# A two-layer decoder's last stage: expert tiles of 128 tokens, sorted in halves of 64, with products by halves of the array

## The chip, the cores and the metric

The kernel runs on one core of a Trainium2 chip. TensorE (PE) multiplies, VectorE (DVE), ScalarE (ACT) and GpSimd (POOL) do the element work, and SyncE (SP) starts most of the transfers. The metric is the device time of one execution in microseconds. An execution under the profiler is also given by its span, from the first to the last instruction.

## The reference

A decoder of two layers works on `x`, 8 sequences of 256 tokens with 256 features, all in float32. Each layer is self-attention, cross-attention and a feed-forward part. Only the last feed-forward part, a mixture of eight experts beside one shared expert, is concerned by the change:

```
a = b * s                                   # 2048 tokens
scores_aE = x_aD @ router_DE                # 8 experts
vals_aK, idx_aK = jax.lax.top_k(scores_aE, 1)
gates_Ea = sigmoid(scores of the chosen expert, -inf for the others).T
routed_in_EaD = gates_Ea[:, :, None] * x_aD[None, :, :]
mid_EaF = silu(routed_in_EaD @ w1_eDF) * (routed_in_EaD @ w3_eDF)      # F = 704
routed_out_EaD = mid_EaF @ w2_eFD
shared_aD = silu(x_aD @ ws1_DF) * (x_aD @ ws3_DF) @ ws2_FD
out_aD = shared_aD + routed_out_EaD.sum(axis=0)
```

`x_aD` is the layer norm of `x`, and the result is added to `x`. Each token has one expert, so a kernel can sort the tokens by expert and give each expert its own tokens only.

## The kernel before

`plain` holds the whole computation. Its earlier stages (self- and cross-attention of layer 0, layer 0's experts, layer 1's self-attention, then `null_cross_attention`) take about 1175 us of the span. The change touches them in two places: `expert_tables` (line 493 on) fills two DRAM tables with zeros, and `reciprocals` (line 979) computes one over the softmax sums of layer 1's cross-attention and counts, in a column of `fit` for each batch, how many lie in a safe range. If a sum anywhere is out of range, a second, general program runs behind this one; `odd_i` carries that flag.

The last stage is `token_experts` (line 1082). It has four parts.

**Routing.** From the scores `sc` (tokens on partitions, 16 columns of 128 tokens) DVE finds each token's expert as a one-hot `hot`. Two matmuls (lines 1153 and 1154) count tokens, `run` adds the counts up over the 16 columns, `over` and `tiles` give each expert's number of 128-token tiles, and `at` the tile at which each expert begins. `pos_i` is each token's row in a table sorted by expert, in which every expert begins at a fresh tile, and `exp_i` is the expert of each tile. With eight experts up to 23 tiles can be needed (`SLOTS`).

**Scatter and shared expert.** GpSimd scatters the normed and gated tokens to their rows in the DRAM table `xs` with 16 indirect transfers (line 1205). Meanwhile PE works on the shared expert: `quarter(q)` makes the hidden layer of 512 tokens, and `joined` multiplies it out and adds it to `x`. Quarters 0 and 1 have their hidden layer from the stage before; quarter 2 is made here, and quarter 3 after the tiles. Behind these comes a small test over `dens`, the softmax sums of the other three attentions, and `fit` (lines 1223 to 1237).

**Tiles.** `slots` walks over the tiles, 19 always and the others behind two branches on the number that is filled. For each tile:

- `fetched(t)` (line 1239) has SP load the tile's 128 rows `xr` (waiting for all 16 scatters), read the tile's expert number, and fetch that expert's weights: `w13`, two transfers of 704 KB and a copy of the last 64 columns by GpSimd (line 790), and `w2`, one of 640 KB and one of 64 KB (lines 799 and 800). Two PE transposes and an ACT copy turn `xr` into `xrT`.
- `into` calls `hidden` (line 818): 11 blocks of 128 weight columns, each multiplied with the tile's 128 tokens in two steps (line 825), then silu on ACT and a product on DVE into `mid_r`.
- `outof` calls `outward` (line 1100): six products over the hidden layer against `w2`'s 256 columns, a copy by ACT, and a store to the DRAM table `ye`, which ACT starts.

The order on PE is written by hand: `fetched(t + 2)`, `into(t + 1)`, `outof(t)`. Weights have three buffers of each kind. SP runs its instructions in order, so a transfer that waits for its buffer holds back those behind it.

**Return.** GpSimd gathers each token's result from `ye` (line 1298) while PE makes quarter 3 of the shared expert; DVE adds, and SP stores the output.

A helper that the change brings into the tiles is already used in the earlier stages: `product` (line 168) issues one product as two, of 64 output partitions each, on the two halves of the array.

Of the kernel before, what the change touches and what calls it, by code (L numbers as in the profile page):

```python
# [50 lines left out]
SLOTS = NT + E - 1  # L51
NEG = -1.0e30
# [14 lines left out]
def plain(ctx: ExitStack, tc: tile.TileContext, a: dict, out: bass.AP, odd_i: bass.AP):  # L67
# [69 lines left out]

    xs = dram.tile([SLOTS * P, D], F32, name="xs")
    ye = dram.tile([SLOTS * P, D], F32, name="ys")

# [350 lines left out]
    def expert_tables():  # L491
        nc.sync.dma_start(gate, a["L0_ffn_gate_w"].rearrange("(c p) e -> p c e", p=P))
        nc.gpsimd.dma_start(experts, a["L0_ffn_experts"].rearrange("e (c p) f -> p e c f", p=P))
        zero = one.tile([P, D], F32, name="zero")
        nc.gpsimd.memset(zero, 0.0)
        nc.gpsimd.dma_start(xs.rearrange("(s p) d -> p s d", p=P), zero.unsqueeze(1).to_broadcast([P, SLOTS, D]))
        nc.gpsimd.dma_start(
            ye[19 * P :].rearrange("(s p) d -> p s d", p=P), zero.unsqueeze(1).to_broadcast([P, SLOTS - 19, D])
        )

        key_i = one.tile([P, E, TOP], I32, name="key_i")
        nc.gpsimd.iota(key_i, [[1, E], [E, TOP]], base=0, channel_multiplier=0)
        key = one.tile([P, S], F32, name="key")
        nc.vector.tensor_copy(key, key_i.rearrange("p e r -> p (e r)"))
        kps = mm.tile([P, 2, 2 * P], F32, tag="mm", name="kps")
        keycol = one.tile([P, 2], F32, name="keycol")
        for h in range(2):
            nc.tensor.transpose(kps[:, h, :P], key[:, bass.ts(h, P)], ident)
        nc.vector.tensor_copy(keycol, kps[:, :, 0])
        for h in range(2):  # L510
            nc.vector.tensor_scalar(later[:, h, :], key, keycol[:, h : h + 1], None, ALU.is_gt)
        num_i = one.tile([P, S], I32, name="num_i")
        nc.gpsimd.iota(num_i, [[1, S]], base=0, channel_multiplier=0)
        nc.vector.tensor_copy(num, num_i)
# [134 lines left out]
    def weights_x():  # L649
# [3 lines left out]
        ctxs = ctx.enter_context(tc.tile_pool(name="ctxs", bufs=2, side="right"))  # L653
        wproj = ExitStack()
        wp = wproj.enter_context(tc.tile_pool(name="wp", bufs=1, side="right"))
# [117 lines left out]
    fit = const.tile([P, B], F32, name="fit")  # L773

    w_l0.close()

# [41 lines left out]
    def hidden(mid, w13, cols, pair, silu):  # L818

        n = cols.shape[2]  # L820
        for i in range(NFC):
            h1, h3 = pair(n)
            for h, lo in ((h1, i * P), (h3, FF + tail + i * P))[: 2 if i < full else 1]:
                for c in range(2):
                    nc.tensor.matmul(h, w13[:, c, lo : lo + P], cols[:, c, :], start=c == 0, stop=c == 1)  # L825
            fw = P
            if i == full:
                fw, h1, h3 = tail, h1[:tail], h1[tail:]
            sl = silu(n)[:fw]
            nc.scalar.activation(sl, h1, AF.Silu)  # L830
            yield nc.vector.tensor_tensor(mid[:fw, i, :n], sl, h3, ALU.mult)  # L831

# [31 lines left out]
    def null_cross_attention(phase):  # L864
# [135 lines left out]

        def divide(oT, rs):
# [29 lines left out]
        def quarter(q):  # L1031
            return hidden(shared["mid_s"][q], shared["ws13"], shared["xnT"][:, :, bass.ts(q, 2 * S)], pair, silu)
# [8 lines left out]
        for b in range(B):  # L1041
# [13 lines left out]
            rs, old = reciprocals(b, den, en), en  # L1055
            if more:
# [25 lines left out]
    def token_experts(phase):  # L1082
        one = phase.enter_context(tc.tile_pool(name="e1", bufs=1))
        work = phase.enter_context(tc.tile_pool(name="e2", bufs=2))
        wts = phase.enter_context(tc.tile_pool(name="e3", bufs=3))
# [3 lines left out]
        xnT, ws13, ws2, mid_s = (shared[n] for n in ("xnT", "ws13", "ws2", "mid_s"))  # L1089

        mid_r = [ended(one.tile([P, NFC, P], F32, name=f"midr{i}")) for i in range(2)]
        w2_r = [ended(one.tile([P, NFC, D], F32, name=f"w2{i}")) for i in range(3)]
# [14 lines left out]
        def quarter(q):  # L1107
            mid = mid_s[q % 2]
            for last in hidden(mid, ws13, xnT[:, :, bass.ts(q, 512)], pair, silu):
                pass  # L1110
            return mid, last
# [5 lines left out]
        mids = [*mid_s]  # L1117


        def row(n, step, name):  # L1120
            i = one.tile([P, n], I32, name=f"{name}_i")
            nc.gpsimd.iota(i, [[step, n]], base=0, channel_multiplier=0)
# [3 lines left out]

        ecol, tcol, jcol = row(E, -1, "ecol"), row(SLOTS, 1, "tcol"), row(NT, P, "jcol")
        nc.vector.tensor_scalar(ecol, ecol, float(E), None, ALU.add)
# [28 lines left out]
        for j in range(NT):  # L1157
            nc.vector.tensor_tensor(run[:, j + 1, :], run[:, j, :], count[:, j, :], ALU.add)
        over = one.tile([P, E, NT], F32, name="overe")
        nc.vector.tensor_tensor(  # L1160
            over,
            run[:, NT, :].unsqueeze(2).to_broadcast([P, E, NT]),
            jcol.unsqueeze(1).to_broadcast([P, E, NT]),
            ALU.is_gt,
        )
        tiles = one.tile([P, E], F32, name="tiles")
        nc.vector.tensor_reduce(tiles, over, AX.X, ALU.add)
        at = one.tile([P, E + 1], F32, name="at")
        nc.vector.memset(at[:, 0:1], 0.0)
        for e in range(E):  # L1170
            nc.vector.tensor_tensor(at[:, e + 1 : e + 2], at[:, e : e + 1], tiles[:, e : e + 1], ALU.add)
        filled_i = one.tile([P, 1], I32, name="filled_i")
        nc.vector.tensor_copy(filled_i, at[:, E : E + 1])
        rows = one.tile([P, E], F32, name="rowse")
        nc.vector.tensor_scalar(rows, at[:, :E], float(P), None, ALU.mult)
        nc.vector.tensor_tensor(run[:, :NT, :], run[:, :NT, :], before, ALU.add)
        nc.vector.tensor_tensor(
            run[:, :NT, :], run[:, :NT, :], rows.unsqueeze(1).to_broadcast([P, NT, E]), ALU.add
        )
        nc.vector.tensor_tensor(run[:, :NT, :], run[:, :NT, :], hot, ALU.mult)  # L1180
        pos = one.tile([P, NT], F32, name="pos")
        nc.vector.tensor_reduce(pos, run[:, :NT, :], AX.X, ALU.add)
        nc.vector.tensor_scalar(pos, pos, SLOTS * P - 1.0, None, ALU.min)
        pos_i = one.tile([P, NT], I32, name="pos_i")
        nc.vector.tensor_copy(pos_i, pos)
        past = one.tile([P, SLOTS, E - 1], F32, name="past")
        nc.vector.tensor_tensor(
            past,
            tcol.unsqueeze(2).to_broadcast([P, SLOTS, E - 1]),
            at[:, 1:E].unsqueeze(1).to_broadcast([P, SLOTS, E - 1]),  # L1190
            ALU.is_ge,
        )
        exp_f = one.tile([P, SLOTS], F32, name="exp_f")
        nc.vector.tensor_reduce(exp_f, past, AX.X, ALU.add)
        exp_i = one.tile([P, SLOTS], I32, name="exp_i")
# [20 lines left out]
        for q in range(3):  # L1216
# [6 lines left out]
            alld = dens.rearrange("p k t h -> p (k t h)")  # L1223
        inside = one.tile([P, 3 * NT * H], F32, name="inside")
        nc.vector.tensor_scalar(inside, alld, 1.0e-25, None, ALU.is_ge)
        nc.vector.scalar_tensor_tensor(inside, alld, 1.0e25, inside, ALU.is_le, ALU.mult)
        ends = one.tile([P, 1], F32, name="ends")
        nc.vector.tensor_reduce(ends, inside, AX.X, ALU.min)
        low = one.tile([P, 2], F32, name="lowe")
        nc.vector.tensor_reduce(low[:, 1:2], fit, AX.X, ALU.min)  # L1230
        nc.vector.tensor_scalar(low[:, 1:2], low[:, 1:2], S - 0.5, None, ALU.is_gt)
        nc.vector.tensor_copy(low[:, 0:1], ends)
        fine = mm.tile([P, 2 * D], F32, tag="mm", name="fine")[:, :2]
        nc.tensor.matmul(fine, ones, low, start=True, stop=True)
        total = one.tile([P, 1], F32, name="total")
        nc.vector.tensor_reduce(total, fine, AX.X, ALU.add)
        nc.vector.tensor_scalar(odd_i, total, 2 * P - 0.5, None, ALU.is_lt)

        def fetched(t):
# [4 lines left out]
            e = nc.sync.value_load(exp_i[0:1, t : t + 1], min_val=0, max_val=E - 1)  # L1244

            def of(n):
                return a[f"L1_ffn_{n}"][bass.ds(e, 1), :, :].rearrange("a p d -> (a p) d")

            w13 = w_in(wts, of("w1_eDF"), of("w3_eDF"), "w13")
            w2 = w_out(w2_r[t % 3], of("w2_eFD"))  # L1250
# [5 lines left out]
            return w13, w2, xrT  # L1256

        def into(t, w13, w2, xrT):
            mid = mid_r[t % 2]
            for _ in hidden(mid, w13, xrT, pair, silu):  # L1260
                pass
            return mid, w2

        def outof(t, mid, w2):
            yr = work.tile([P, D], F32, tag="yr", name="yr")
            nc.scalar.copy(yr, outward(mid, w2, 0))
            nc.scalar.dma_start(ye[bass.ts(t, P), :], yr)

        def slots(lo, hi):


            with tc.manual_schedule(engines={mybir.EngineType.PE}):
                got = {lo: fetched(lo), lo + 1: fetched(lo + 1)}
                ahead = into(lo, *got.pop(lo))
                for t in range(lo, hi):
                    now = ahead
                    if t + 2 < hi:
                        got[t + 2] = fetched(t + 2)
                    if t + 1 < hi:
                        ahead = into(t + 1, *got.pop(t + 1))  # L1280
                    outof(t, *now)


        slots(0, 19)
        filled = nc.values_load(filled_i[0:1, 0:1], min_val=NT, max_val=SLOTS)
        with tc.If(filled > 19):
            slots(19, 21)
            with tc.If(filled > 21):
                slots(21, SLOTS)
# [964 lines left out]
```

## Time and profile before

| | |
|---|---|
| Time, median of 3 runs | 1417.21 us (1416.78 to 1418.94) |
| Profiled execution | 1420.55 us, span 1418.5 us, granted clock 0.992 |
| Scatters to `xs` on POOL | 1193.28 to 1213.4 us of the span |
| First weights sent by SP | 1191.94 us |
| First transpose of a tile | 1227.3 us |
| Last product out of a tile ends | 1374.8 us |
| Quarter 3 of the shared expert begins | 1376.79 us |
| Last product of the span ends | 1408.6 us |

In the page and the answers that follow, a group of instructions is named by line, engine, operation, output and inputs, then the shape. "128*128" after a matmul is the part of the array that it uses (rows * columns), so "128*64" uses half of the columns. A float32 product appears as two records. PE is the multiplying, PEld the loading of weights beside it. A timeline line gives the start, the length and the number of instructions merged into it. A line of windows gives the stretch, its length, the busy time of PE, PEld, DVE, ACT and POOL with the number of instructions, the granted clock, the share of time in which the core's DMA engines were busy, and GB/s.

### The profile page before, as it was taken

What the parts mean: (1) busy time and instruction counts of PE and PEld (TensorE: products, weight loads), DVE (VectorE), ACT (ScalarE), POOL (GpSimd) and SP (SyncE); (2) the same over time, 40 slices, a digit from 0 to 9 for tenths busy, and PEclk for the clock granted to TensorE, in tenths of its full rate; (3) what the DMA queues carried; (4) which work ended last, traced back from release to release, by engine and by line L of the source; (5) the groups of instructions that cost most, each with busy time, mean ns of one, the idle gap of its engine ahead of it and who ended that gap; (6) DMA issues with size and microseconds to landing.
All of it is one profiled execution on the core that took longest, in us unless ns stands there. A gap on an engine that the chain in (4) does not pass through costs nothing. (4 is left out here: it accounts for less than half of the span.)

```text
span 1418.5 us, 23533 instructions
## 1 busy us (share of the span) xinstructions
PE 1372.8 (97%) x9514; PEld 974.4 (69%) x9514; DVE 498.9 (35%) x1477; ACT 462.9 (33%) x754; POOL 387.1 (27%) x487
## 2 busy tenths in 40 slices
PE   6999999999999999999999999999999999999997
PEld 3666756756766666676677767667677656799974
DVE  6343553653655744410131312122131325222212
ACT  2555444444443434423131313223131311132220
POOL 4132142142143244212141424324141523100013
PEclk8999999999999999999999999999999999999999
DMA  9000000000000005010101101010101103589943
GB/s 306 27 12 16 16 17 8 16 16 1 2 9 1 9 1 216 2 62 16 45 2 44 31 15 31 15 31 16 31 2 30 30 0 128 182 302 318 314 134 110
DMA packets 54553, 91.05 MB, mean 64 GB/s; under 512 B 6160, under 2 KB 38720, under 8 KB 52896
## 3 DMA queue, kind: packets, MB, share of 16 engines
q1 hardware_dynamic: 47360, 70.00, 15.8%
q0 software_dynamic: 4064, 16.13, 3.1%
q10 hardware_dynamic: 3008, 3.28, 0.6%
q8 instruction: 79, 1.29, 0.4%
q14 instruction: 42, 0.34, 0.1%
HBM read 79.03 MB, written 10.37 MB: 63 GB/s over the span
## 5 line engine op out<-in xcount | busy, mean ns | idle before, releaser
L260 PE MATMUL o<-pT,padv 128*64 128x256 f32 (+1 forms) x1536 | 171.6, 365 | 1.1 <-POOL pT L240 1.1
L237 ACT ACTIVATE pT<-st 128x1024 f32<-128x1024 f32 (+1 forms) x128 | 110.7, 916 | 88.7 <-PE st L228 87.9
L260 PEld LDWEIGHTS o<-pT,padv 128*64 128x64 f32 x1536 | 103.1, 137 | 52.6 <-issue 10.1
L228 PE MATMUL st<-qm,kT 64*128 64x256 f32 (+1 forms) x1024 | 117.2, 367 | 1.6 <-DVE qm L206 1.4
L874 PE MATMUL fm<-ctxT,wkv_x 128*128 128x256 f32 x512 | 112.1, 379 | 0.0
L897 PE MATMUL vps<-wkv_x,ctxT 128*128 128x512 f32 x256 | 111.7, 594 | 0.0
L228 PEld LDWEIGHTS st<-qm,kT 64*128 64x128 f32 x1024 | 90.0, 189 | 26.8 <-issue 15.1
L874 PEld LDWEIGHTS fm<-ctxT,wkv_x 128*128 128x128 f32 x512 | 96.6, 190 | 12.8
L825 PE MATMUL h<-xrT,w 128*128 128x128 f32 x836 | 96.6, 275 | 0.2 <-ACT xrT L1255 0.2
L825 PEld LDWEIGHTS h<-xrT,w 128*128 128x128 f32 x836 | 94.9, 192 | 0.5 <-ACT xrT L1255 0.5
L933 POOL TENSOR_TENSOR both<-pTx 128x512 f32<-128x512 f32 x64 | 79.4, 1272 | 52.1 <-ACT pTx L931 33.0
L931 ACT ACTIVATE pTx<-stx 128x1024 f32<-128x1024 f32 x64 | 62.1, 1023 | 90.0 <-PE stx L927 90.0
L897 PEld LDWEIGHTS vps<-wkv_x,ctxT 128*128 128x128 f32 x256 | 48.2, 190 | 57.5 <-issue 57.4
L237 ACT ACTIVATE pT<-st,kbias 128x1024 f32<-128x1024 f32 x64 | 68.1, 1115 | 28.7 <-PE st L228 28.6
L830 ACT ACTIVATE sl<-h 128x128 f32<-128x128 f32 (+1 forms) x126 | 38.8, 308 | 115.6 <-PE h L825 106.7
L152 POOL TENSOR_TENSOR lnrs<-lnve,mhalf 128x2 f32<-128x2 f32 x48 | 34.0, 710 | 154.3 <-DVE lnve L150 102.8
L831 DVE TENSOR_TENSOR midr<-sl,h 128x128 f32<-128x128 f32 x114 | 32.9, 288 | 109.9 <-ACT sl L830 61.1
L228 PE MATMUL st<-qm,memk 64*128 64x256 f32 x512 | 68.8, 393 | 0.5
L927 PE MATMUL stx<-qTx,kTx 64*128 64x256 f32 x512 | 64.3, 391 | 2.5 <-ACT pTx L931 2.5
L147 DVE BATCH_NORM_STATS2 lxst<-yx 128x6 f32<-128x256 f32 x16 | 6.0, 418 | 162.1 <-ACT yx L1015 162.1
L170 PE MATMUL qk<-l_wqkv,xnT 128*64 128x512 f32 x256 | 62.3, 608 | 0.7 <-ACT xnT L180 0.7
L240 POOL TENSOR_SCALAR_AFFINE_SELECT pT<-pT 128x512 f32<-128x512 f32 x64 | 40.1, 646 | 81.8 <-ACT pT L237 78.5
(260 smaller groups left out, 2125.9 us busy)
## 6 DMA issues: line engine op xcount, KB each, us to landing
w<-L_ffn_w_eDF SPq DMA_DIRECT2D x38, 704.0 KB
w<-L_ffn_w_eFD SPq DMA_DIRECT2D x19, 640.0 KB
rs<-rd SPq DMA_DIRECT2D x16, 512.0 KB
ctxT<-ctx_T SPq DMA_DIRECT2D x8, 512.0 KB
wkv_x<-L_xattn_Wkv POOLq DMA_DIRECT2D x1, 4096.0 KB
xs<-zero POOLq DMA_DIRECT2D x1, 2944.0 KB
xr<-xs SPq DMA_DIRECT2D x19, 128.0 KB
ys<-yr ACTq DMA_DIRECT2D x19, 128.0 KB
```

The source lines that it names most:

```text
L170: nc.tensor.matmul(out[h], lhsT[:, h], rhs, start=start, stop=stop, skip_group_check=True)
L228: nc.tensor.matmul(st[:, g, i, :n], kT[rows, c, bass.ts(kt, P)], qm[rows, 2 * mq + i, c, q0:], start=True, stop=True,)
L237: nc.scalar.activation(pT[:, :, :, :n], st[:, :, :, :n], AF.Exp, scale=scale, **kb)
L240: nc.gpsimd.affine_select(out=pT[:, :, :, :P], in_=pT[:, :, :, :P], compare_op=ALU.is_ge, fill=0.0, base=0, pattern=[[0, 2], [0, 2], [1, P ...
L260: nc.tensor.matmul(o[64 * i : 64 * i + 64, mq, q0:], v_pad[:, kt, 4 * c + 2 * mq + i, 2 * g : 2 * g + 2, :], pTs[kt][:, g, i, : S - q0], s ...
L825: nc.tensor.matmul(h, w13[:, c, lo : lo + P], cols[:, c, :], start=c == 0, stop=c == 1)
L830: nc.scalar.activation(sl, h1, AF.Silu)
L874: nc.tensor.matmul(ps[:, i, :], w[:, cc, (c2 + i) * P : (c2 + i + 1) * P], rows[:, cc, :], start=cc == 0, stop=cc == n - 1,)
L897: nc.tensor.matmul(ps.rearrange("p h d -> p (h d)"), ctxT[:, cc, bass.ts(t, P)], wkv_x[:, cc, lo : lo + 8 * XD], start=cc == 0, stop=cc == ...
L927: nc.tensor.matmul(st[:, g, kt, :], kT[rows, c, bass.ts(kt, P)], qT[rows, c, :], start=True, stop=True)
L931: nc.scalar.activation(pT, st, AF.Exp, scale=scale)
L933: nc.gpsimd.tensor_tensor(both, pT[:, :, 0, :], pT[:, :, 1, :], ALU.add)
```

## The change

Tokens are sorted in half tiles of 64. An expert's whole tiles of 128, where a last part of more than 64 counts as whole, come first, expert after expert; the experts' last parts of at most 64 follow behind them, one half tile each. Whatever the counts, at least 12 tiles are whole, so tiles 0 to 11 (`PAIRED`) have one expert; each later tile has an expert number for each of its halves, and fetches two sets of weights. 17 tiles always run, in an order that puts a tile with two experts after each two with one; up to three more lie behind branches. The tables shrink from 23 to 20 tiles.

In `into`, each product is issued through `product`, by halves of the array; for a tile with two experts it is done for each expert with that expert's 64 token columns. `outof` multiplies by halves too, each half of 64 tokens with its own expert's `w2`. The products of the shared expert stay as they were. Weights have four buffers of each kind; to make room, the pool `ctxs` is given back with the projection weights of the stage before.

The test over `dens` moves out of the last stage into `null_cross_attention`, behind the reciprocals of batch 1, where it counts into three more columns of `fit`.

```diff
+TILES = NT + E // 2
+PAIRED = NT - E // 2
...
-        ctxs = ctx.enter_context(tc.tile_pool(name="ctxs", bufs=2, side="right"))
         wproj = ExitStack()
+        ctxs = wproj.enter_context(tc.tile_pool(name="ctxs", bufs=2, side="right"))
...
+        def in_range():
+            for k in range(3):
+                v = dens[:, k].rearrange("p t h -> p (t h)")
+                low = work.tile([P, S], F32, tag="low", name="lowk")
+                nc.vector.tensor_scalar(low, v, 1.0e-25, None, ALU.is_ge)
+                nc.vector.scalar_tensor_tensor(
+                    low, v, 1.0e25, low, ALU.is_le, ALU.mult, accum_out=fit[:, B + k : B + k + 1]
+                )
...
-        wts = phase.enter_context(tc.tile_pool(name="e3", bufs=3))
+        wts = phase.enter_context(tc.tile_pool(name="e3", bufs=4))
...
-        w2_r = [ended(one.tile([P, NFC, D], F32, name=f"w2{i}")) for i in range(3)]
+        w2_r = [ended(one.tile([P, NFC, D], F32, name=f"w2{i}")) for i in range(4)]
...
+        nc.vector.tensor_scalar(ends_at[:, 0, :], pairs, 2.0 * half, None, ALU.mult)
+        nc.vector.tensor_scalar(ends_at[:, 1, :], far, half, None, ALU.mult)
+        nc.vector.tensor_scalar(ends_at[:, 2, :], begin[:, 0, :], half, None, ALU.mult)
+        left = one.tile([P, NT, E], F32, name="left")
+        nc.vector.tensor_tensor(left, rank_in, each(ends_at[:, 0, :]), ALU.is_ge)
+        nc.vector.tensor_tensor(left, left, each(ends_at[:, 1, :]), ALU.mult)
+        nc.vector.tensor_tensor(rank_in, rank_in, each(ends_at[:, 2, :]), ALU.add)
+        nc.vector.tensor_tensor(rank_in, rank_in, left, ALU.add)
...
+            sets = []
+            for i in [t] if t < PAIRED else [2 * t - PAIRED, 2 * t - PAIRED + 1]:
+                e = nc.sync.value_load(exp_i[0:1, i : i + 1], min_val=0, max_val=E - 1)
...
+                w13 = w_in(wts, of("w1_eDF"), of("w3_eDF"), "w13")
+                ring.append(ring.pop(0))
+                sets.append((w13, w_out(ring[-1], of("w2_eFD"))))
...
+        def into(t, sets, xrT):
+            mid_r.append(mid_r.pop(0))
+            mid, n = mid_r[-1], P // len(sets)
+
+            def first(h, lo):
+                for i, (w13, _) in enumerate(sets):
+                    for c in range(2):
+                        product(h[:, bass.ts(i, n)], w13[:, c, lo : lo + P], xrT[:, c, bass.ts(i, n)], c == 0, c == 1)
...
+        def outof(t, mid, sets):
+            ps = mm.tile([P, 2 * D], F32, tag="mm", name="out")[:, :D]
+            for i in range(NFC):
+                for k, h in enumerate((slice(0, 64), slice(64, P))):
+                    nc.tensor.matmul(
+                        ps[h], mid[:, i, h], sets[k % len(sets)][1][:, i, :], start=i == 0, stop=i == NFC - 1, skip_group_check=True
+                    )
...
-        slots(0, 19)
+        slots([0, 1, 12, 2, 3, 13, 4, 5, 14, 6, 7, 15, 8, 9, 16, 10, 11])
+        more = nc.values_load(filled_i[0:1, 0:1], min_val=2 * NT, max_val=2 * TILES - 1)
+        with tc.If(more > 34):
+            slots([17])
+            with tc.If(more > 36):
+                slots([18, 19])
```

## The prediction

> **What bounds the kernel now.** I read the page first (PE busy 97%), then the chain of waits, then the last stage by itself: windows of ten microseconds, the timeline of PE, and that of SP's queue.
>
> ```profile
> PE 1372.8 (97%) x9514; PEld 974.4 (69%) x9514; DVE 498.9 (35%) x1477; ACT 462.9 (33%) x754; POOL 387.1 (27%) x487
> ...
> w<-L_ffn_w_eDF SPq DMA_DIRECT2D x38, 704.0 KB
> w<-L_ffn_w_eFD SPq DMA_DIRECT2D x19, 640.0 KB
> ```
>
> ```profile
> 1241.17 5.08 PE L825 MATMUL h<-xrT,w 128*128 128x128 f32 x44
> 1246.09 2.76 PE L1103 MATMUL out<-w,midr 128*128 128x256 f32 x12
> 1248.68 0.38 PE L1253 MATMUL xrp<-ident,xr 128*128 128x128 f32 x2
> 1248.90 1.28 PE L825 MATMUL h<-xrT,w 128*128 128x128 f32 x10
> ```
>
> From start to start a tile costs PE 4.92 us into the hidden layer (44 records, two for each f32 product), 2.59 us out of it and 0.22 us of transposes: 7.73 us. The tiles run from 1227.3 (first transpose) to 1374.8 (last product out), 147.5 us, which is 19 x 7.73 = 146.9 and a start. So PE bounds this stage. But the transfers stand close behind:
>
> ```profile
> 1250.00:1260.00 10.00, 10.00 (x81) 9.64 (x80) 2.60 (x9) 2.93 (x12) 0.29 (x1) 1.00 0.88 304
> 1260.00:1270.00 10.00, 10.00 (x78) 9.57 (x77) 2.54 (x9) 3.09 (x11) 0.29 (x1) 1.00 0.97 322
> 1300.00:1310.00 10.00, 10.00 (x71) 9.41 (x71) 2.28 (x8) 2.58 (x9) 0.29 (x1) 1.00 1.00 355
> ```
>
> The last two columns are the DMA share and GB/s. Over the ten windows from 1250 to 1350 the share averages 0.92. Each tile fetches a whole set of expert weights: 704 KB three times, 2.163 MB, and moves 0.131 MB of rows in and as much out: 2.425 MB in 7.73 us are 314 GB/s, which the windows' mean is. What the engines can do shows where SP sends transfers without a pause (1193 to 1206):
>
> ```profile
> 1196.00:1197.00 1.00, 1.00 (x6) 0.90 (x5) 0.42 (x1) 0.00 (x0) 0.96 (x1) 1.00 1.02 332
> 1197.00:1198.00 1.00, 1.00 (x7) 0.87 (x6) 0.00 (x0) 0.00 (x0) 0.72 (x1) 1.00 0.98 251
> 1198.00:1199.00 1.00, 1.00 (x6) 0.89 (x5) 0.22 (x1) 0.00 (x0) 0.69 (x2) 1.00 0.97 318
> ...
> 1202.00:1203.00 1.00, 1.00 (x6) 0.87 (x6) 0.00 (x0) 0.00 (x0) 0.69 (x2) 1.00 1.03 413
> ```
>
> About 300 GB/s while w2 (rows of 1 KB) passes, 414 while w13 (rows of 2.8 KB) does. So w13 takes 1.442/0.414 = 3.5 us, w2 0.721/0.30 = 2.4 us, a **set 5.9 us**, and a tile's rows 0.262/0.30 = 0.87 us: 6.77 us a tile before, against 7.73 of PE.
>
> **What the Trainium skill says.** "DMA: Bandwidth & Descriptors", Where 436 GB/s comes from, has about 358 GB/s bind reads from HBM; the 413 above differ, and the measurement decides. "TensorEngine Tiling (Array Packing)", Key Properties, says that tiles load weights and multiply in parallel and that a change of the tiling mode drains TensorE. The trace agrees with the first: 16 records by halves, each 256 columns, take 1.93 us, (1.93 - 0.38)/15 = 103 ns each where the full array takes 216. On the second, the half-array product after full transposes begins 0.2 us after the last of them where 0.11 is usual: 0.1 us a change. "TensorE: Matmul & The Clock Gate", LDWEIGHTS, prices a load by its columns over 1.2 GHz: 107 ns for 128, 53 for 64; the 4.92/44 = 112 ns above fit a load and a product side by side. The same page's first table gives PE a queue of 64; that matters below.
>
> **The change part by part.** *How many tiles.* The reference's own arithmetic on its inputs, up to the router, gives the experts 325, 377, 367, 187, 190, 249, 168 and 185 tokens: 19 tiles of 128 (as the trace has), or 34 halves of 64, exactly the 17 tiles that always run; the two best scores of a token are at least 0.0004 apart, so no count should move. Twelve tiles have one expert, five have two. **22 sets are fetched instead of 19.**
>
> *PE, single tile.* 88 half-array records of 128 columns at 107/2 = 53 ns are 4.7 us; a mixed run of 16 half records of 256 and 128 columns takes 1.52 us, which leaves the short ones 50 to 65 ns, so 4.4 to 5.7. I take 4.75. Out: 24 records x 103 ns = 2.48 us. Transposes 0.22, two mode changes 0.2. Sum 7.65 us, as before.
>
> *PE, tile of two experts.* Twice the weights over 64 columns each: 176 half-array records. No row shows 64 columns. The nearest are 8 columns:
>
> ```profile
> 139.31 0.66 PE L177 MATMUL tr<-ident,att 128*128 128x128 f32 x4
> 139.90 0.64 PE L170 MATMUL lg<-gate,xnT 128*64 128x8 f32 x16
> 140.38 1.93 PE L260 MATMUL o<-pT,padv 128*64 128x256 f32 x16
> ```
>
> (0.64 - 0.20)/15 = 29 ns for a load and a product, so two halves load at once. Streaming 64 columns is 53 ns a half, 27 ns a record with two halves. Best case 176 x 28 = 4.9 us. Worst: 16 records are 32 instructions, which fit the queue of 64 and may have stood ready, so a long run may cost what a 53 ns load for each record costs: 176 x 53 = 9.4 us. I take 4.9 and keep 9.4. Then PE alone needs 12 x 7.65 + 5 x 7.8 = 131 us, 16.5 less than before.
>
> *DMA.* 22 x 5.9 + 17 x 0.87 = 144.6 us, before 128.6. A group of the new order (two single tiles, one double) needs 4 x 5.9 + 3 x 0.87 = 26.2 us of transfers and 23 of PE: **the stage turns from PE to DMA.** At 1227.8 three sets had landed before; the fourth buffer lets a fourth follow at once. From there 19 sets (112.1 us), 13 row reads and 16 writes (12.5) remain: 124.6 us. Early the four buffers are full and SP's queue waits in order: w2 of set 5 for the first tile's product out (at +13.0, transfers free at +9.9, 1.3 us from issue to data: 4.4 us lost), set 6 likewise 1.9, set 7 1.7: 8 us. From +30 the buffers come free before SP gets to them. The last w2 lands at 124.6 + 8 + 0.5 = +133; the last w13 is 2.4 us earlier, and after it and its copied tail (0.5) come one tile in and two out, 4.9 + 5.0: +141. Stage about **141.5 us, 6.0 less**.
>
> *Routing.* Added on DVE: about nine [128x8] operations of 0.16, three [128x128] of 0.28, second halves of over and past and longer sums, some 3.8 us; the dens test leaves (0.56 + 0.94 + 0.96 and small ones, 2.6 us). Net +1.2 us to pos_i, the 16 scatters (POOL, 1.27 us apart) and xr behind them. xr was sent at 1215.0 and its transposes ran at 1227.3, as PE was busy with the shared expert until then: hidden, with 10 us to spare. in_range puts six operations of 0.4 to 0.5 us on DVE behind the reciprocals of batch 1, where DVE next waits some 8 us for rs: nothing. POOL's three more tail copies (0.29) lie in its idle time; the fourth w2's memset is 0.44 us at 1175. Less zeroing and the smaller final test: nothing on the path. SP's waits are in the DMA sum; ACT's ys queue is as before.
>
> Sum: the profiled execution took 1420.55 us (span 1418.5), 3.3 above the median of 1417.21. Less 6.0: 1414.5, or **1411.2** by the median.
>
> **Rivals.**
> 1. *The transfers end it, as above:* 1411.2, own range 1407 to 1414.4. For: share 0.92 and 16% more bytes of weights. Chance 0.40.
> 2. *PE still bounds:* transfers run at 414 throughout; 131 us and a small start: 16 less, 1401. For: full-busy seconds of this stage reach 400 and more. Against: w2's and the rows' 1 KB pieces were never that quick. Chance 0.08.
> 3. *The transfers take it all:* at 5% lower rates (two queues and three sizes mixed) the same count ends at 146: within 0.2% of the median (2.8 us, about what a measurement of this kernel can tell from no change). Chance 0.18.
> 4. *Slower: half-array loads don't sustain.* One mechanism, in the five double tiles: a load and a product of 64 columns at 53 ns a record. Then PE needs 12 x 7.65 + 5 x 12.3 = 153.3 and a start and a stall, 154.5: 7 us slower, 1424. It decides from about 45 ns a record (5 x (2.9 + 7.9) + 92 = 146). For: only bursts of 16 are seen at 29 ns, and instruction fetch would share full queues; against: the bursts. Chance 0.33. That a count differs by one half and an 18th tile runs behind the branch, at over 8 us, I hold at 0.01, within the slower chance of 0.34.
>
> **Numbers.** Faster 0.48 (1 and 2), same 0.18, slower 0.34. Range 1402 to 1426: from nearly all of the second case to the price of the fourth.
>
> **What would show it.** Right: 17 xr loads and 22 sets; DMA share at or above 1.0 from about 1260 to 1355; PE stalls of 3 to 4 us ahead of each double tile, with w behind them; last product out near 1369. Rival 4: PE without stalls, double tiles above 10 us each. Rival 2: 7.7 us tiles throughout. Wrong altogether: the first transpose later than 1229, or a wait on routing or buffers ahead of it.

## The result and the profile after

Over four runs each, the kernel before takes 1416.99 us (1416.06 to 1418.94) and the changed one 1425.2 us (1424.38 to 1427.34): a ratio of 1.0059, with a 95% interval of 1.0046 to 1.0071. The change costs 8.2 us where 6.0 were to be won. The profiled execution of the changed kernel took 1425.63 us, with a span of 1423.9 us and a granted clock of 0.987.

The first part of the page, to be set beside the line shown of before:

```profile
PE 1366.9 (96%) x10790; PEld 953.7 (67%) x10790; DVE 497.8 (35%) x1484; ACT 458.6 (32%) x738; POOL 387.1 (27%) x493
...
w<-L_ffn_w_eDF SPq DMA_DIRECT2D x44, 704.0 KB
w<-L_ffn_w_eFD SPq DMA_DIRECT2D x22, 640.0 KB
```

PE is busy 5.9 us less in a span 5.4 us longer: work was removed and waits came in. The 44 loads of w13 are the 22 sets that were counted ahead. The loss lies in the tiles. Their first transpose is at 1226.61 (before 1227.3) and the last product out ends at 1376.42 + 5.35 = 1381.8, so the stage takes 155.2 us; before it took 147.5. (From the start of quarter 3 to the end of the span the profile of the changed kernel is 2.5 us shorter, 39.2 against 41.7, so the span grows by less than the stage and the gap behind it.) The double tiles are 12 to 16, in this order. PE's timeline (start, length, instructions; in brackets the idle time ahead and what ended it) at tiles 13, 14 and 16 and at the end:

```profile
1269.01 4.65 PE L172 MATMUL h<-xrT,w 128*64 128x64 f32 x152 [1.53 <-DMA w<-L_ffn_w_eDF]
...
1296.90 0.69 PE L1304 MATMUL xrp<-ident,xr 128*128 128x128 f32 x2 [4.82 <-DMA xr<-xs]
1297.52 7.69 PE L172 MATMUL h<-xrT,w 128*64 128x64 f32 x176
...
1354.18 0.69 PE L1304 MATMUL xrp<-ident,xr 128*128 128x128 f32 x2 [5.55 <-DMA xr<-xs]
1354.80 6.48 PE L172 MATMUL h<-xrT,w 128*64 128x64 f32 x176
...
1376.42 5.35 PE L1326 MATMUL out<-w,midr 128*64 128x256 f32 x48
```

Twice PE stands still for about 5 us ahead of two transposes, and what ends the wait is not a weight but `xr`, the 128 KB of rows of a tile. These are the transposes for the tile *after* the double tile: the hand-written order on PE is `fetched(t + 2)`, `into(t + 1)`, `outof(t)`, and the two transposes belong to `fetched`. The double tile's products, which need nothing of these rows, stand behind them. In the queue of SP (start, length) one sees why the rows are late:

```profile
1285.09 0.40 SPq L792 DMA_DIRECT2D w<-L_ffn_w_eDF  x1
1285.68 0.39 SPq L793 DMA_DIRECT2D w<-L_ffn_w_eDF  x1
1286.26 0.61 SPq L803 DMA_DIRECT2D w<-L_ffn_w_eFD  x1
1287.35 0.47 SPq L804 DMA_DIRECT2D w<-L_ffn_w_eFD  x1
1289.77 0.35 SPq L1289 DMA_DIRECT2D xr<-xs  x1
```

The last line sends the rows of tile 6, which follows double tile 14. They are sent only when SP is through with the double tile's two sets, and the transposes that wait for them start at 1296.90, 7.1 us later. PE had been free since 1289.32 + 2.76 = 1292.08. Tile 14's own second set was complete at 1294.24, when GpSimd copied the tail of its w13:

```profile
1294.24 0.29 POOL L794 COPY w<-w 128x128 f32<-128x128 f32 x1 [6.58 <-DMA w<-L_ffn_w_eDF]
```

So of the 4.82 us up to 2.2 might have been a wait for weights even with the rows in time, and some 2.7 are the rows' alone. At tile 16 it is alike: PE is free at 1348.63, the second set is complete at 1351.71, and the transposes start at 1354.18. Only two of the five double tiles stop for rows. SP's order, unlike PE's, is not written by hand: the rows that follow double tiles 12, 13 and 15 were sent 13 us or more before their transposes (those of tile 4 at 1239.68, for transposes at 1266.20), and only those of tiles 6 and 10 are sent so late.

The windows (stretch, length, busy PE, PEld, DVE, ACT, POOL, granted clock, DMA share, GB/s):

```profile
1230.00:1240.00 10.00, 10.00 (x160) 8.92 (x156) 2.89 (x10) 3.10 (x11) 0.29 (x1) 1.00 0.62 202
...
1270.00:1280.00 10.00, 10.00 (x216) 8.73 (x213) 2.31 (x8) 3.04 (x11) 0.29 (x1) 1.00 1.05 368
1290.00:1300.00 10.00, 5.18 (x68) 3.90 (x66) 0.42 (x2) 1.02 (x3) 0.29 (x1) 0.79 1.05 367
...
1350.00:1360.00 10.00, 5.82 (x140) 5.49 (x142) 0.86 (x4) 1.49 (x5) 0.59 (x2) 0.83 1.07 355
```

Where PE loses half of its time the DMA engines are full, so the averages would read as "the transfers bound it". What was waiting in them, and for what, only the chain of waits and the queue tell. The clock's column shows a second loss: after the two stops it is 0.79 and 0.83, and the hidden layer of tile 14 takes 7.69 us and that of tile 16 6.48, where 5.35 is usual (experiment 3 below).

### The profile page after: what moved, and what is told of

Same layout as the page of the kernel before. It is cut to its first block, busy times and chain, and to the rows that moved or that the text cites. A ratio compares the mean times of both kernels' runs of the same rounds, so it can differ in the third digit from the quotient of the medians.

```text
span 1423.9 us, 26049 instructions
## 1 busy us (share of the span) xinstructions
PE 1366.9 (96%) x10790; PEld 953.7 (67%) x10790; DVE 497.8 (35%) x1484; ACT 458.6 (32%) x738; POOL 387.1 (27%) x493
## 5 line engine op out<-in xcount | busy, mean ns | idle before, releaser
L887 PEld LDWEIGHTS fm<-ctxT,wkv_x 128*128 128x128 f32 x512 | 96.6, 190 | 12.8
L172 PE MATMUL h<-xrT,w 128*64 128x128 f32 (+1 forms) x1936 | 91.1, 257 | 4.0 <-DMA w<-L_ffn_w_eDF 2.2
L172 PEld LDWEIGHTS h<-xrT,w 128*64 128x64 f32 x1936 | 87.3, 144 | 7.7 <-issue 4.5
L832 ACT ACTIVATE sl<-h 128x128 f32<-128x128 f32 (+1 forms) x114 | 35.4, 310 | 118.0 <-PE h L172 64.1
L833 DVE TENSOR_TENSOR midr<-sl,h 128x128 f32<-128x128 f32 x102 | 29.4, 288 | 121.2 <-PE h L172 114.6
```

The lines of the kernel that those rows point to most:

```text
L172: nc.tensor.matmul(out[h], lhsT[:, h], rhs, start=start, stop=stop, skip_group_check=True)
L887: nc.tensor.matmul(ps[:, i, :], w[:, cc, (c2 + i) * P : (c2 + i + 1) * P], rows[:, cc, :], start=cc == 0, stop=cc == n - 1,)
```

## The experiments

The batches ran on two chips, on which the kernel before took 1417.3 and 1424.6 to 1425.9 us, so only ratios to the kernel before on the same chip are compared. The changed kernel stands at 1.0059; it was not timed on the second chip, and the kernel before was not profiled there.

The theory from this profile: **the rows of the next tile**, queued behind two sets of weights and ahead of the double tile in PE's order, cost the two stops of 5 us and the clock behind them. Its rivals: the transfers as such (a cure of the rows would only turn the wait into one for weights), and half-array products that don't keep their rate, the prediction's fourth case.

**1. Rows on another queue.** In the changed kernel the row loads go out from GpSimd instead of SP:

```diff
-            get = nc.sync.dma_start(xr, xs[bass.ts(t, P), :])
+            get = nc.gpsimd.dma_start(xr, xs[bass.ts(t, P), :])
```

> The changed kernel, with one edit: a tile's rows xr are loaded on GpSimd's queue instead of SP's. Theory A (bandwidth): the 22 sets and the rows are the same bytes, so the stage ends where it did: 1423 to 1427 us. Theory B (one queue): the rows of a tile stand behind two sets of weights in SP's queue, which kept PE idle for 4.8 and 5.5 us ahead of two double tiles, slowed its clock after them, and kept SP itself waiting for a row buffer from 1228 to 1238: 1412 to 1418 us, with no wait for xr left in the tiles.

Measured: 1415.94 us, ratio 0.9987 (0.9978 to 0.9996); the stage takes 146.0 us (1228.8 to 1374.8). One line brings back 9 to 10 us. PE's timeline around tile 14:

```profile
1295.39 0.69 PE L172 MATMUL h<-xrT,w 128*64 128x64 f32 x16 [1.47 <-DMA w<-L_ffn_w_eDF]
...
1297.38 6.20 PE L172 MATMUL h<-xrT,w 128*64 128x64 f32 x152 [1.31 <-DMA w<-L_ffn_w_eDF]
```

Both waits for rows are gone after the first tile. In their place come short waits for the double tile's own weights, 0.2 to 1.5 us each, 5.4 us in all (six waits), where the changed kernel waited 4.82 + 5.55 us for rows and 1.53 + 0.71 for weights. The rival of the transfers holds for what is left, not for the loss. The clock still falls once: the 152 records at 1297.38 take 6.20 us where 4.65 is usual.

**2. Rows where they were, transposes later.** The two transposes and the ACT copy leave `fetched` and come after the hidden layer of the next tile; no queue is changed:

```diff
+            return sets, xr
+
+        def turned(sets, xr):
             ps = mm.tile([P, 2, 2 * P], F32, tag="mm", name="xrp")
...
                         ahead = into(order[i + 1], *got.pop(order[i + 1]))
+                    if i + 2 < len(order):
+                        got[order[i + 2]] = turned(*got[order[i + 2]])
                     outof(t, *now)
```

> The changed kernel, with one edit: the transposes of the tile after next come behind the hidden layer of the next tile instead of ahead of it; the rows stay on SP's queue. Theory A: no change, 1423 to 1427 us. Theory B in its narrow form (PE's written order makes a double tile wait for rows that only the tile after it needs): the double tiles 14 and 16 begin 2 to 3 us earlier each and with less slow clock, 1417 to 1421 us.

Measured: 1417.41 us, ratio 1.0006 (0.9996 to 1.0016); the stage takes 146.4 us. The rows still arrive late, but nothing stands behind them:

```profile
1292.48 0.87 PE L172 MATMUL h<-xrT,w 128*64 128x64 f32 x24
1294.50 4.65 PE L172 MATMUL h<-xrT,w 128*64 128x64 f32 x152 [1.15 <-DMA w<-L_ffn_w_eDF]
1299.08 0.44 PE L1307 MATMUL xrp<-ident,xr 128*128 128x128 f32 x2
```

Tile 14's products begin at 1292.48, and the transposes for tile 6 follow at 1299.08, with no wait; their rows were again sent late, at 1290.46. Experiment 1 changes more than this dependence, as SP no longer waits for the scatters and sends four sets ahead of the tiles. Experiment 2 leaves that as it was and gains nearly the same, so the stall was the written order on PE meeting late rows.

**3. One set for a double tile.** Both halves use the first expert's weights:

```diff
-            for i in [t] if t < PAIRED else [2 * t - PAIRED, 2 * t - PAIRED + 1]:
+            for i in [t] if t < PAIRED else [2 * t - PAIRED]:
...
-            return sets, xrT
+            return sets if t < PAIRED else 2 * sets, xrT
```

> The changed kernel, with the second expert of each double tile left out: both halves are multiplied with the first expert's weights, so 17 sets are fetched instead of 22 and PE's work is the same. Theory A and B: PE is never kept waiting by weights, 12 tiles of 7.9 and 5 of 8.2 us, the stage takes about 137 us instead of 155: 1406 to 1409 us. Theory C (half-array products cost PE the loss): over 1418 us.

Measured: 1408.12 us, ratio 0.9946 (0.9927 to 0.9966). PE does what it does in the changed kernel, without the five extra sets:

```profile
1265.84 5.35 PE L172 MATMUL h<-xrT,w 128*64 128x64 f32 x176
1271.02 2.76 PE L1326 MATMUL out<-w,midr 128*64 128x256 f32 x24
```

A double tile's hidden layer takes 1271.02 - 1265.84 = 5.18 us, 29 ns a record over 176 records. The fourth case's 9.4 us is refuted; that its 1424 lies near the result is chance, and so is it that the range, drawn up to this case's price, holds the result. The stage takes 139.3 us here, without a wait for a transfer: the second sets cost 155.2 - 139.3 = 15.9 us in the changed kernel, and PE's own work saves 8.2 of the 147.5.

**4. Halves without the new tiles.** The kernel before, with the tiles' products by halves of the array:

```diff
-                    nc.tensor.matmul(h, w13[:, c, lo : lo + P], cols[:, c, :], start=c == 0, stop=c == 1)
+                    if halves:
+                        halves(h, w13[:, c, lo : lo + P], cols[:, c, :], c == 0, c == 1)
...
-            nc.scalar.copy(yr, outward(mid, w2, 0))
+            for i in range(NFC):
+                product(ps, mid[:, i, :], w2[:, i, :], i == 0, i == NFC - 1)
+            nc.scalar.copy(yr, ps)
```

> The kernel before, with its 19 tiles multiplied by halves of the array into and out of the hidden layer; transfers as before. Theory C, sized from the two traces (7.91 against 7.73 us a tile): 19 x 0.18 = 3.4 us slower than before, 1420 to 1421 us. If the difference in the traces is due to the transfers and not to the halves: within 1 us of before, 1416 to 1418 us.

Measured: 1420.23 us, ratio 1.0020 (1.0012 to 1.0028), 2.8 us for 19 tiles, 0.15 us a tile. The timeline of one tile:

```profile
1239.95 5.02 PE L170 MATMUL h<-xrT,w 128*64 128x128 f32 x88
1244.81 2.76 PE L170 MATMUL out<-w,midr 128*64 128x256 f32 x24
1247.50 0.44 PE L1256 MATMUL xrp<-ident,xr 128*128 128x128 f32 x2
1247.87 5.02 PE L170 MATMUL h<-xrT,w 128*64 128x128 f32 x88
```

From start to start 4.86 us go into the hidden layer, 2.69 out of it, 0.37 into transposes and the change of mode: 7.92, where the full array takes 7.73.

**5. Both cures, the buffers, and whole products for single tiles.** Experiment 5 is 1 and 2 together. Experiment 6 adds full-array products for tiles with one expert. Experiment 7 is 5 with a fifth buffer for w13 and six for w2: two of its own and four views in the hidden layers of the shared expert, which are free during the tiles. Experiment 8 is all of it.

```diff
+                        if len(sets) == 1:
+                            nc.tensor.matmul(h, w13[:, c, lo : lo + P], xrT[:, c, :], start=c == 0, stop=c == 1)
+                            continue
...
-        wts = phase.enter_context(tc.tile_pool(name="e3", bufs=4))
+        wts = phase.enter_context(tc.tile_pool(name="e3", bufs=5))
...
+        ring = [*w2_r, *(mid_s[i][:, :, lo : lo + D] for i in (1, 0) for lo in (0, D))]
```

> The changed kernel with both edits: rows on GpSimd's queue and transposes behind the next hidden layer. If each edit cures the same stall (a double tile kept waiting for the rows of the tile behind it), the two do no more than one: 1414 to 1417 us. If they cure different losses, they add: 1407 to 1410 us.

> As e5, and the tiles with one expert go through the whole array again, into and out of the hidden layer; double tiles stay by halves. If PE's own work decides the stage now: 12 x 0.18 = 2.2 us below e5. If the transfers decide it: within 1 us of e5, as PE only waits longer ahead of the double tiles.

> As e5, with five buffers for w13 and six for w2 instead of four (four of the w2 buffers lie in the shared expert's two hidden-layer buffers, which stand idle between quarter 1 or 2 and quarter 3). If what is left is the transfers' pause while all four buffers are full (share 0.48 to 0.76 from 1230 to 1260, some 10 us): 4 to 7 us below e5, with shorter stops ahead of the double tiles. If the transfers' rate alone decides: within 1 us of e5.

> As e7, with single tiles through the whole array. If buffers take the transfers off the path, PE decides, and this is about 2 us below e7 and 1404 to 1409 us, near the run that fetches only 17 sets (1408). If they don't: within 1 us of e7.

Measured, on the second chip:

| Run | us | Ratio (95%) | First transpose | Stage, us |
|---|---|---|---|---|
| 5, both cures | 1426.87 | 1.0013 (1.0003 to 1.0023) | 1234.9 | 143.9 |
| 6, and full singles | 1427.16 | 1.0020 (1.0004 to 1.0035) | 1235.7 | 144.8 |
| 7, 5 and more buffers | 1420.33 | 0.9965 (0.9954 to 0.9976) | 1234.1 | 139.9 |
| 8, all | 1420.37 | 0.9966 (0.9955 to 0.9978) | 1235.1 | 137.5 |

The buffers shorten the stage by 4 us. The two cures together were to reach 0.998 to 1.000 if they share one stall, or 0.993 to 0.995 if they add; 1.0013 is neither, as the tiles begin late (below). By the stage, 143.9 against 146.0 and 146.4, both together gain 2 us on one of them, where two separate losses of 9 us would have added: they share one stall. The whole products change no time, 6 against 5 or 8 against 7, but the stage of 8 is 2.4 us shorter than that of 7, near the 12 x 0.18 expected; a stop of PE in quarter 3, 3.57 us in 8 and 1.32 in 7, took it back. The buffers end the waits for weights (7 and 8 show none in the tiles); with five and six of them and all 22 sets the stage takes 139.9 us, where it took 139.3 with only 17 sets in experiment 3. So it isn't the rate of the transfers that bounds the rest with four buffers, but that they go in order and can't run further ahead. And something new holds these runs: the tiles begin 7 to 9 us later than in the changed kernel. Of the timeline of the last, three engines:

```profile
1215.91 0.42 DVE L1139 TENSOR_TENSOR x<-x,out 128x256 f32<-128x256 f32 x1 [13.78 <-remote]
1215.95 1.08 ACT L832 ACTIVATE sl<-h 128x512 f32<-128x512 f32 x2 [30.06 <-remote]
1216.60 7.64 PE L840 MATMUL h<-xnTe,ws 128*128 128x512 f32 x12 [7.22 <-ACT sl L832]
```

ACT and DVE resume within 0.04 us of each other, and PE, which needs ACT's result, 0.7 us later; ACT and DVE show no wait for anything on this core that would fit. The stop lies in the shared expert's quarter 2, ahead of the tiles.

**6. Where the late start comes from.** Three runs on the same chip. Experiment 9 is 8 with the rows back on SP. Experiment 10 is 8 with the third set of weights held until the last scatter. Experiment 11 is the kernel before with experiment 1's line.

```diff
+                if t == 12 and not sets:
+                    tc.add_manual_dep(shared["loads"][-1].ins, puts[-1].ins.name, landed, reason="held back")
```

> As e8, with the rows back on SP's queue (whose first wait for the scatters pauses the transfers from about 1206 to 1216 us). In e5 to e8 PE, ACT and DVE all stood still for 6 to 7 us around 1211 to 1218 with nothing that they waited for in the trace, while the transfers were at a share of 1.05. Theory I (instructions are fetched by the same engines, and starve while a long run of weights fills them): the first transpose comes back from 1235 to about 1227, and the time is 0.5 to 0.7% below e8's: 0.990 to 0.993 of the kernel before. Theory II (that stop belongs to the chip or to the instruction layout, not to the transfers): as e8, 0.996 to 0.998.

> As e8 (rows on GpSimd's queue), with one wait added: the weights of the third set are sent only once the last scatter has landed. Theory I: the stop ahead of the tiles goes and the first transpose runs at about 1227: 0.989 to 0.993 of the kernel before. Theory II: as e8, 0.996 to 0.998, or slower as the weights come later.

> The kernel before, with its rows on GpSimd's queue, so that its three sets of weights follow each other without SP's wait for the scatters. Theory I: its first transpose comes later, 1230 us or more, with PE standing still around 1205 to 1215: 2 to 6 us slower than before. Theory II: within 1 us of before.

Measured: experiment 9 takes 1416.2 us, ratio **0.9940** (0.9918 to 0.9962), the lowest ratio of all, below both kernels; experiment 10's 0.9948 can't be told from it, and both lie just above the 0.993 that theory I allowed. It has no stop ahead of the tiles, and its first transpose is early:

```profile
1229.82 0.66 PE L1308 MATMUL xrp<-ident,xr 128*128 128x128 f32 x4 [0.40 <-DVE x L1139]
```

Experiment 11 takes 1430.88 us, ratio 1.0035 (1.0019 to 1.0051): the same one line that cured the changed kernel makes the kernel before slower, by the 2 to 6 us of theory I, and its trace has the stop:

```profile
1215.58 7.96 PE L825 MATMUL h<-xnTe,ws 128*128 128x512 f32 x12 [5.36 <-issue]
```

Experiment 10 takes 1418.75 us, ratio 0.9948 (0.9931 to 0.9965). Its stop was to go and didn't: PE stood still from 1209.4 to 1216.7, and the first transpose was at 1234.43. So on this chip the stop ahead of the tiles goes with the rows' queue: all six runs there with rows on GpSimd had it, of 5.4 to 7.3 us on PE, the one with rows on SP did not. On the other chip experiment 1 had rows on GpSimd and no stop.

The queue is not the whole of it. In quarter 3, behind the tiles, all seven runs on this chip have another stop of PE (1.3 to 3.7 us), experiment 9 among them:

```profile
1396.20 10.16 PE L1128 MATMUL out<-ws,mid 128*128 128x256 f32 x38 [3.70 <-issue]
```

There ACT and DVE stand still with it. None of the other profiles has more than 0.33 us in that place. As the kernel before was not profiled on this chip, it may have such stops too; its time there, 7 to 9 us above the other chip's, leaves room for them.

The theory was that the engines' instructions are held up while transfers fill the DMA engines: with the rows on SP, SP waits for the scatters, and the share falls to 0.30 from 1210 to 1215 in the kernel before and to 0.29 in experiment 9, while in experiment 11 it stays at 1.05. Against the simple form of it speak experiment 10, with a share of 0.26 from 1210 to 1215 (though 1.01 to 1.02 in the fifteen microseconds before), and the stop in quarter 3 of experiment 9, with a share of 0.25 from 1392 to 1396. The trace does list instruction loads among the DMA packets; for the changed kernel:

```profile
q8 instruction: 89, 1.46, 0.4%
q14 instruction: 42, 0.34, 0.1%
```

It doesn't say which engine such a load served or whether it was waited for, so the cause stays open.

## Why the prediction failed, step by step

**Counts, routing, start: right.** 17 row loads, 22 sets, first transpose at 1226.6, within 1229. The first weights are sent at 1194.21 (before 1191.94) and the first scatter at 1194.87 (before 1193.28), 1.6 us later where 1.2 was counted: it stays hidden.

**Rates of transfers: right.** Full windows show 335 to 371 GB/s; 5.9 us a set and 0.87 for a tile's rows make 26.2 us for a group's 4 x 2.163 + 3 x 0.262 = 9.44 MB, which is 360 GB/s; the two full windows with a stop of PE show 367 and 355.

**Double tile on PE: right in kind.** 29 ns a record, 5.18 us for the hidden layer where 4.9 was taken.

**PE's other terms: too small.** A single tile takes 7.91 us, not 7.65: out of the hidden layer 2.69 (112 ns a half record, not 103), into it 4.86 (4.75), transposes and change of mode 0.37 (0.42). A double tile takes 5.18 + 2.69 + 0.37 = 8.24, not 7.8. That is 12 x 0.26 + 5 x 0.44 = 5.3 us on the sum of 131, and with the transposes at the start (0.9) and two stops of PE that wait for nothing shown (1.81 and 0.62 us) it comes to 139.6, where experiment 3 has 139.3. The gain of PE was half of what was counted. The 103 came from a burst of 16 records whose length was read off one line; a run of 24 shows the sustained rate.

**The step that failed** is the one that let only the double tile's own weights hold it up: stalls of 3 to 4 us "ahead of each double tile, with w behind them". For the rows the sum asked once, for the first tile ("hidden, with 10 us to spare"), and then charged them 0.87 us of transfer a tile and no latency. With one set a tile, the rows were sent more than a tile ahead of need, and that cover was taken for granted. With two sets in front of them in the same queue they were sent at 1289.77, and their transposes started at 1296.90, and PE's written order asks for them *before* the double tile's products. The Trainium skill, "DMA: Bandwidth & Descriptors", Queues, rings and completion order, says that each DMA engine takes a queue's descriptors in order; the 7.1 us here agree with that. Of the 15.9 us that the second sets cost, 4.82 + 5.55 are these two waits (of which up to 2.2 and 3.1 might have been waits for weights with the rows in time), and 2.3 + 1.1 the lower clock of the products behind them. What falls to double tiles without a row in the way, the 1.53 and 0.71 us at tiles 13 and 15 and no wait for weights at 12, is less than the 3 to 4 us that each was to lose.

"TensorE: Matmul & The Clock Gate", Part 1, puts TensorE at half its clock after an idle window of about 3.4 us. Both stops are longer, and the granted clock behind them, 0.50 from 1297 to 1302 and from 1354 to 1357, agrees. But one such stop isn't needed: in experiment 1 the clock was 0.50 from 1298 to 1301 too, after stops of 1.47 and 1.31 us with 0.69 us of work between them.

A second sentence failed with it: "From +30 the buffers come free before SP gets to them." In the changed kernel SP's loads of w2 (L803) waited for a tile's last products to free their buffer through the whole stage; only two of the eleven waits, 8.4 us, end before 1262, +35:

```profile
SPq L803 <- PE out L1326: 39.5, 11, 7.0
```

**The early loss: the wait was right, a part was missed.** 8 us were to be lost as the w2 of sets 5, 6 and 7 wait for a tile's products out. They did: they were sent at 1241.50, 1250.05 and 1257.95, as those of tiles 0, 1 and 12 ended. What the sum put at nothing is SP's own work. Before it sends set 5, it sends three row loads, and between and behind them it reads the expert numbers of later tiles from memory, one after the other:

```profile
1227.05 4.50 SPq L1289 DMA_DIRECT2D xr<-xs  x3
L1294 SPq TENSOR_LOAD <-exp_i x18: 262/267/273, 1227.8 to 1240.1; - x18
1238.60 0.39 SPq L792 DMA_DIRECT2D w<-L_ffn_w_eDF  x1
```

Seventeen of the eighteen reads lie ahead of set 5, 0.57 us from start to start. The buffer of its w13 was free when tile 0's hidden layer ended, at 1232.5; SP sent it at 1238.60, and the share from 1230 to 1240 is 0.62. What was expected of experiment 1 put this stretch down to a wait for a row buffer; the trace shows none. The kernel before makes 16 such reads in a row, but from 1222.1 to 1230.6, before its next buffer is free, and experiment 9, with three reads there and the others spread over the stage, has a share of 1.06 from 1230 to 1240. No experiment moved the reads alone, so what they cost is not shown.

The last w13's tail is copied at 1364.45 where about 1359 was counted, and the stage ends at 1381.8 instead of 1369, 12.8 us late: 5.5 from the weights, and 7.3 because PE, held up at tile 16, was a further tile behind when they came. Experiment 1 gives back 7 of it (its stage ends at 1374.8); experiments 5 and 7 (stage 143.9 and 139.9) show that buffers are most of what is left. With the rows out of the way, the likeliest case's mechanism, double tiles that wait for their weights, is what experiment 1's trace shows, at 146.0 us where 141.5 was counted.

**The end.** The gap to quarter 3 grew from 1.99 to 2.94 us. From there to the last product the two profiles take 31.8 and 31.1 us, and from there to the end 9.9 and 8.1; no experiment looked into the latter.

## What to carry to other kernels

When a change makes one item of an in-order queue larger, look at what stands *behind* it in that queue and where the consumer's fixed order asks for it: a small load that nobody has looked at can hold up work that doesn't need it, and the DMA share will look like a bandwidth limit. Cost a sustained product from a long run of it, not from a burst. A queue's own small work counts too: look for what its engine does between two transfers. An edit that cures one kernel (rows on another queue) may hurt its neighbour, so the queue and the order are to be tried apart; here moving the consumer and adding buffers, with the rows left on SP (experiment 9, which also has whole products for single tiles), had the lowest ratio.

## What the runs showed of the hardware

- A stop of about 5 us of PE costs more than itself: the clock behind it was 0.50 for a few microseconds, and the products took 2.3 and 1.1 us longer. Two stops of 1.3 and 1.5 us, 0.7 us apart, did the same (1.55 us, experiment 1).
- Reading one expert number into a register keeps SP busy for 0.57 us; seventeen in a row kept it from sending a set whose buffer had been free for 6 us.
- Half-array records of 64 columns hold 29 ns over 176 in a row; records of 256 columns hold 112 ns, so two cost 224, where a full-array record takes 216.
- In and just behind double tiles PE stops for 0.2 to 1.8 us at places where it waits for nothing that the profile shows (1.54 in the changed kernel at tile 12, 1.81 in experiment 3); two such stops remain even when no transfer is late.
- PE, ACT and DVE stood still together for 5 to 7 us, while GpSimd went on, in all six runs with rows on GpSimd on one chip, and not in the one such run on the other. The DMA share was 0.90 to 1.03 from 1195 to 1205 and 1.01 to 1.06 from 1205 to 1210, ahead of the stop. A shorter stop, of 1.3 to 3.7 us, came behind the tiles in all seven runs on that chip. The cause is open.
